# One chain per batch for the flow layer and the router of a two-layer decoder

## The chip, the cores and the metric

The kernel runs on one core of a Trainium2 chip. The core has five engines that run side by side, each with its own queue in strict order: TensorE (PE in the profile, with its weight loads as PEld), VectorE (DVE), ScalarE (ACT), GpSimd (POOL) and SyncE (SP), which here only starts transfers. The metric is the device time of one execution in microseconds, the median of several runs.

## The reference

Sixteen batches of 256 tokens with 256 channels go through two decoder layers: self-attention, cross-attention, a product-key layer, banded attention, the flow layer (`_L1_xattn_ref`) and a mixture of experts (`_L1_ffn_ref`). Each is applied to the layer norm of x, and its result is added to x. The last two are what the change touches (c is the normalised x, q is the context of 120 rows):

```python
cq = jnp.einsum('bcd,bqd,d->bcq', c, q, w_cq) + b_cq
s = (c @ w_c + b_c)[:, :, None] + (q @ w_q + b_q)[:, None, :] + cq
a = jax.nn.softmax(s, axis=2)
c2q_att = jnp.einsum('bcq,bqd->bcd', a, q)
b_att = jax.nn.softmax(jnp.max(s, axis=2), axis=1)
q2c_att = jnp.einsum('bc,bcd->bd', b_att, c)[:, None, :]
x = jnp.concatenate([c, c2q_att, c * c2q_att, c * q2c_att], axis=-1)
z = x @ W_l.T + b_l
...
logits = jnp.einsum('bsd,de->bse', input_emb, Wr) + br
route_w = jax.nn.softmax(logits, axis=-1)
_, topk_idx = jax.lax.top_k(route_w, TOP_K)
mask = jax.nn.one_hot(topk_idx, E, dtype=route_w.dtype).sum(-2)
routed = route_w * mask
routed = routed / routed.sum(axis=-1, keepdims=True)
h = jax.nn.relu(jnp.einsum('bsd,edh->ebsh', input_emb, W1) + b1[:, None, None, :])
expert_out = jnp.einsum('ebsh,ehd->ebsd', h, W2) + b2[:, None, None, :]
return jnp.einsum('bse,ebsd->bsd', routed, expert_out)
```

There are eight experts, and each token goes to the best two. All is float32.

## The kernel before

x stays in SBUF as sixteen tiles `xt[b]` of 128 partitions x 2 x 256. The layers follow one another, each over all batches. A framework places the instructions of an engine by what they depend on and adds the waits; inside a `manual_schedule` block, the engines named there keep the order of the program.

**Flow layer (L871 to L964).** `layernorm_stats` (L98 to L102) takes the statistics of all 32 halves of batches. Then a loop runs over the batches: two loads, `cx` (L883) and `cT` (L885), by SP; `qc` (L889) on DVE; the row of context terms `pr` (L894) and `qrow` (L896); the normalised x (L108), its transposes (L131) and their copy (L132); for each half, the scores `p_s` (L143, L145), their maximum `nm` (L906), the exponential `e` (L909), its scaling (L911), transpose (L913) and copy (L914); the attended context `pc` (L917); the second softmax over the maxima (`pm` L930, `low` L932, `be` L935, `pb` L940, `batt` L942), `pd` (L946) and `q2c` (L954). Four pairs of channel blocks form `xcat`: x, attended context (L924), their product (L925) and x scaled by `q2c` (L956). For each half, the output is a bias product (L959) and eight products with `wl` (L961), added to x by L964. A float32 product of 256 columns shows as two matrix instructions. `wl` itself is loaded ahead of the attention before it (L818).

**Router (L971 to L1080).** The statistics again, all 32 halves into one tile `xr` (L1009), transposes (L131), and products of eight columns, for each half a bias row (L143) and two channel blocks (L145). When those of all batches are there, the softmax (L1022 to L1027), the best two experts (`max` L1031, `max_index` L1032, `pick` L1038, `either` L1043) and the ranks are worked out for all tokens at once: two products of 256 columns (L1048) and a running sum over the 32 halves on DVE (`ahead`, L1052 to L1058). `place` is a token's row in the scratch array `rows`, where each expert has a region of 4096 rows, and `sloti` the same as an integer (L1078).

**Scattering (L1085).** Sixty-four indirect transfers on POOL's queue, each of 128 rows of 1040 bytes, write `xr` to `rows`. Beside them DVE works out the list of 39 tiles of 256 tokens: `full` (L1096), `need`, `ends` (L1107), `et`, the integer `eti` (L1123), and the rows that each tile gathers (`source`, L1145).

**Output biases (L1149 to L1158).** For each half, the routing weights are transposed (L1150), copied (L1152) and multiplied with `b2` (L1154); the result is added to x (L1155), and SP writes the batch to the output (L1158).

**Experts (L1161 on).** For each tile SP reads the expert's number and loads its weights `wt`, 2052 KB, into one of two buffers (L1165); POOL gathers the tokens from `rows` (L1173); then transposes (L1180), 16 + 16 products (L137, L1211), and an accumulating scatter to the output (L1220).

Of the kernel before, what the change touches and what calls it, by code (L numbers as in the profile page):

```python
# [12 lines left out]
U32 = mybir.dt.uint32  # L13
# [5 lines left out]
P = 128  # L19
# [32 lines left out]
def tile_decoder(ctx: ExitStack, tc: tile.TileContext, a: dict, out: bass.AP, last: int = 6):  # L52
# [762 lines left out]
    with ExitStack() as st:  # L815
        w4 = pool(st, "w4")
        wl = T(w4, [P, 8, D], "wl")
        nc.sync.dma_start(wl, a["l1x_w"].rearrange("(c p) e -> p c e", p=P))  # L818
        s4 = st.enter_context(ExitStack())
        w5 = pool(s4, "w5")  # L820
# [11 lines left out]
        wk = pool(s4, "wk4", 2)  # L832
        ps = pool(s4, "ps4", 2, PSUM)
        ps2 = pool(s4, "sc4", 1, PSUM)
# [36 lines left out]
        s4.close()  # L871
        if last == 4:
            return done()

        wk = pool(st, "wk5", 2)

        ps = pool(st, "ps5", 2, PSUM)
        layernorm_stats(wk)
        bsum = T(w4, [1, 1], "bsum")
        nc.vector.tensor_reduce(bsum, row(R_SC, 3), AX.X, ALU.add)  # L880
        for b in range(B):
            cx = T(wk, [NQ, D], "cx")
            nc.sync.dma_start(cx, a["ctx"][b])  # L883
            cT = T(wk, [P, 2, NQ], "cT")
            nc.sync.dma_start(cT, a["ctxT"][b].rearrange("(c p) q -> p c q", p=P))  # L885

            qc = T(wk, [P, 2, NQ], "qc")
            for dc in range(2):
                nc.vector.tensor_scalar(  # L889
                    qc[:, dc, :], cT[:, dc, :], col(C_WCQ + dc), col(C_WC + dc), ALU.mult, ALU.add  # L890
                )
            pr = T(ps, [1, NQ], "row")
            for dc in range(2):
                nc.tensor.matmul(pr, lhsT=col(C_WQ + dc), rhs=cT[:, dc, :], start=dc == 0, stop=dc == 1)  # L894
            qrow = T(wk, [1, NQ], "qrow")
            nc.vector.tensor_scalar(qrow, pr, bsum, None, ALU.add)  # L896

            xn = normalized(wk, b)
            xcat = T(wk, [P, 8, S], "xcat")
            transposed(ps, xn, xcat[:, 0:2, :])  # L900
            nm = T(wk, [P, 2], "nm")
            aT = T(wk, [NQ, 2, P], "aT")
            for t in range(2):
                p_s = T(ps, [P, NQ], "t2")
                project_rows(p_s, xcat, slice(t * P, (t + 1) * P), qc, 0, NQ, qrow)
                nc.vector.tensor_reduce(nm[:, t : t + 1], p_s, AX.X, ALU.max, negate=True)  # L906
                e = T(wk, [P, NQ], "e")
                z = T(wk, [P, 1], "z")
                nc.scalar.activation(e, p_s, AF.Exp, bias=nm[:, t : t + 1], accum_out=z)  # L909
                nc.vector.reciprocal(z, z)  # L910
                nc.vector.tensor_scalar(e, e, z, None, ALU.mult)  # L911
                pt = T(ps, [NQ, P], "t1")
                nc.tensor.transpose(pt, e, ident)  # L913
                nc.scalar.copy(aT[:, t, :], pt)  # L914
            pc = T(ps, [P, 2, S], "t2")
            for dc in range(2):
                nc.tensor.matmul(  # L917
                    pc[:, dc, :],
                    lhsT=cx[:, dc * P : (dc + 1) * P],
                    rhs=aT.rearrange("p t n -> p (t n)"),  # L920
                    start=True,
                    stop=True,
                )
            nc.scalar.copy(xcat[:, 2:4, :], pc)  # L924
            nc.vector.tensor_tensor(xcat[:, 4:6, :], xcat[:, 0:2, :], pc, ALU.mult)  # L925


            pm = T(ps, [1, 2, P], "row")
            for t in range(2):
                nc.tensor.matmul(pm[:, t, :], lhsT=nm[:, t : t + 1], rhs=ident, start=True, stop=True)  # L930
            low = T(wk, [1, 1], "low")
            nc.vector.tensor_reduce(low, pm, AX.XY, ALU.min)  # L932
            be = T(wk, [1, 2, P], "be")
            bz = T(wk, [1, 1], "bz")
            nc.scalar.activation(be, pm, AF.Exp, bias=low, scale=-1.0, accum_out=bz)  # L935
            nc.vector.reciprocal(bz, bz)
            nc.vector.tensor_scalar(be, be, bz, None, ALU.mult)
            pb = T(ps, [P, 2], "row")
            for t in range(2):
                nc.tensor.matmul(pb[:, t : t + 1], lhsT=be[:, t, :], rhs=ones[:, 0:1], start=True, stop=True)  # L940
            batt = T(wk, [P, 2], "batt")
            nc.vector.tensor_copy(batt, pb)  # L942
            pd = T(ps, [P, 2], "row")
            for dc in range(2):
                for t in range(2):
                    nc.tensor.matmul(  # L946
                        pd[:, dc : dc + 1],
                        lhsT=xn[:, t, dc * P : (dc + 1) * P],
                        rhs=batt[:, t : t + 1],
                        start=t == 0,  # L950
                        stop=t == 1,
                    )
            q2c = T(wk, [P, 2], "q2c")
            nc.vector.tensor_copy(q2c, pd)  # L954
            for dc in range(2):
                nc.vector.tensor_scalar(xcat[:, 6 + dc, :], xcat[:, dc, :], q2c[:, dc : dc + 1], None, ALU.mult)  # L956
            for t in range(2):
                y = T(ps, [P, D], "t2")
                nc.tensor.matmul(y, lhsT=ones, rhs=row(R_BL, D), start=True, stop=False)  # L959
                for c in range(8):  # L960
                    nc.tensor.matmul(  # L961
                        y, lhsT=xcat[:, c, t * P : (t + 1) * P], rhs=wl[:, c, :], start=False, stop=c == 7
                    )
                nc.vector.tensor_add(xt[b][:, t, :], xt[b][:, t, :], y)  # L964
    if last == 5:
        return done()
# [5 lines left out]
    with ExitStack() as st:  # L972
        w6 = pool(st, "w6")
        ws = pool(st, "ws", 2)
        wk = pool(st, "wk6", 2)
        s6 = st.enter_context(ExitStack())
        ps = pool(s6, "ps6", 2, PSUM)

        wr = T(w6, [P, 2, NE], "wr")
        nc.scalar.dma_start(wr, a["m_wr"].rearrange("(c p) e -> p c e", p=P))  # L980
        b2 = T(w6, [NE, D], "b2")
        nc.scalar.dma_start(b2, a["m_b2"])

# [14 lines left out]
        before_me = T(w6, [P, P], "before_me")  # L998
        nc.vector.tensor_scalar(before_me, along, part, None, ALU.is_gt)
        all_ones = T(w6, [P, P], "all_ones")  # L1000
        nc.vector.memset(all_ones, 1.0)

        layernorm_stats(wk)
        xr = T(w6, [P, NT, RW], "xr")
        pl = T(ps, [P, NT, NE], "lg", bufs=1)
        for b in range(B):
            for t in range(2):
                i = 2 * b + t
                nc.vector.tensor_scalar(  # L1009
                    xr[:, i, 0:D], xt[b][:, t, :], mv[:, i, 0:1], rstd[:, i : i + 1], ALU.subtract, ALU.mult  # L1010
                )
            xT = T(wk, [P, 2, S], "xT")
            transposed(ps, xr[:, 2 * b : 2 * b + 2, 0:D], xT)
            for t in range(2):
                project_rows(pl[:, 2 * b + t, :], xT, slice(t * P, (t + 1) * P), wr, 0, NE, row(R_BR, NE))

        def over(tile_):
            return tile_.unsqueeze(2).to_broadcast([P, NT, NE])

        red = T(w6, [P, NT], "red")  # L1020
        rw = T(w6, [P, NT, NE], "rw")
        nc.vector.tensor_reduce(red, pl, AX.X, ALU.max)  # L1022
        nc.vector.tensor_tensor(rw, pl, over(red), ALU.subtract)
        nc.scalar.activation(rw, rw, AF.Exp)
        nc.vector.tensor_reduce(red, rw, AX.X, ALU.add)
        nc.vector.reciprocal(red, red)
        nc.vector.tensor_tensor(rw, rw, over(red), ALU.mult)  # L1027
        top = T(w6, [P, NT, 8], "top")
        topi = T(w6, [P, NT, 8], "topi", U32)
        for i in range(NT):  # L1030
            nc.vector.max(out=top[:, i, :], in_=rw[:, i, :])  # L1031
            nc.vector.max_index(out=topi[:, i, :], in_max=top[:, i, :], in_values=rw[:, i, :])  # L1032
        first = T(w6, [P, NT, 2], "first")
        nc.vector.tensor_copy(first, topi[:, :, 0:2])
        picks = []
        for k in range(2):
            pick = T(w6, [P, NT, NE], f"pick{k}")
            nc.vector.tensor_tensor(  # L1038
                pick, over(first[:, :, k]), iota8.unsqueeze(1).to_broadcast([P, NT, NE]), ALU.is_equal
            )  # L1040
            picks.append(pick)
        either = T(w6, [P, NT, NE], "either")
        nc.vector.tensor_add(either, picks[0], picks[1])  # L1043


        pr = T(ps, [P, 2, NT, NE], "rank", bufs=1)
        for i, w in enumerate((before_me, all_ones)):
            nc.tensor.matmul(pr[:, i], lhsT=w, rhs=either, start=True, stop=True)  # L1048
# [298 lines left out]
```

## Time and profile before

| | us |
|---|---|
| three runs | 3927.28, 3928.51, 3930.91 |
| profiled execution | 3936.24 |
| its span, first to last instruction | 3934.5 |
| end of attention (last x add, L386), from the span's start | 2851.3 |
| first cx load of the flow layer | 2851.4 |
| first scores p_s of the flow layer | 2871.0 |
| last x add of the flow layer (L964) | 3161.2 |
| integer list of tiles eti | 3258.6 |
| first load of wt issued | 3260.9 |
| last scatter issued (L1085) | 3334.2 |
| first expert product (L137) | 3346.7 |

Over the whole span PE is busy for 3504.4 us, DVE 2275.2, POOL 1589.4 and ACT 1538.1. A busy PE is not a PE at its peak: products are pipelined and their ends are modelled, and TensorE's clock is granted in steps, so the same product takes twice as long at half clock. A row of the windows gives, for a stretch of the span, the busy time of each engine with its number of instructions, then TensorE's granted clock, the share of time in which the DMA engines were busy, and what they moved. A row of a timeline gives start, duration, engine, line, operation, output and inputs, and in brackets how long the engine was idle before and what ended that.

### The profile page before, as it was taken

The numbers are of one execution on the slowest core, as the hardware profiler recorded it, in microseconds if no ns is written. First come the engines' busy times: TensorE is split into PE (matmuls) and PEld (weight loads), VectorE is DVE, ScalarE is ACT, GpSimd is POOL, SyncE is SP. The second block draws the span as 40 slices with busy tenths as digits, with TensorE's granted clock in tenths as the row PEclk, the third lists the DMA queues.
The fourth block names the chain that finished last, engine by engine and source line by source line (L and its number), as shares of the span: only waits on it lengthen the run. The fifth ranks groups of instructions, "written<-read, shape, count | busy, mean of one in ns | idle before, by whom it ended". The sixth has DMA issues, their size and how long they took to land.

```text
span 3934.5 us, 130886 instructions
## 1 busy us (share of the span) xinstructions
PE 3504.4 (89%) x57612; PEld 2876.7 (73%) x57612; DVE 2275.2 (58%) x9061; ACT 1538.1 (39%) x2704; POOL 1589.4 (40%) x1551
## 2 busy tenths in 40 slices
PE   6999999659999999999999987999879983999998
PEld 3666777448888888888888875676556671788887
DVE  6777533498888888888888733444343331111111
ACT  2455566434444444444444324555411110232232
POOL 2333200036666666666666633444300006233332
PEclk8999999879999999999999997999889855999999
DMA  9200000200000000000000000000000004465564
GB/s 334 86 2 2 5 9 8 93 3 4 4 4 4 4 4 4 4 4 4 4 4 4 4 27 1 1 2 2 2 17 14 11 6 171 141 190 178 172 187 132
DMA packets 49325, 182.00 MB, mean 46 GB/s; under 512 B 14889, under 2 KB 36785, under 8 KB 42354
## 3 DMA queue, kind: packets, MB, share of 16 engines
q1 hardware_dynamic: 29840, 144.22, 10.4%
q0 software_dynamic: 18048, 29.14, 3.5%
q8 instruction: 452, 7.41, 0.8%
q14 instruction: 119, 0.97, 0.1%
q10 hardware_dynamic: 866, 0.26, 0.0%
HBM read 150.66 MB, written 57.15 MB: 53 GB/s over the span
## 4 chain that ended last, share of the span: by engine, by line
PE 66%; DVE 25%; POOL 3%; ACT 3%; issue 2%; another core or an unknown queue 1%; DMA 0%; ACTq 0%; POOLq 0%; DVEq 0%
PE acc L758 8%; PE sa L246 7%; PE h L137 7%; PE t L145 7%; DVE hot L714 7%; PE y L1211 7%; PE hid L137 6%; PE t L733 4%; PE t L961 3%; PE t L347 3%; POOL hot L721 3%; DVE q L274 2%; PE t L137 2%; PE t L228 2%; PE sb L246 2%
## 5 line engine op out<-in xcount | busy, mean ns | idle before, releaser
L721 POOL TENSOR_TENSOR hot<-hot,w 104x1024 f32<-104x1024 f32 x256 | 523.1, 2043 | 295.9 <-DVE hot L714 192.0
L714 DVE TENSOR_TENSOR hot<-wij,iota 104x1024 f32<-104x1024 f32 x512 | 599.2, 1213 | 52.9 <-ACT w L704 44.0
L137 PE MATMUL hid<-xnT,w_dn 128*128 128x128 f32 x4096 | 525.3, 281 | 5.5 <-issue 5.3
L137 PEld LDWEIGHTS hid<-xnT,w_dn 128*128 128x128 f32 x4096 | 483.8, 193 | 17.9 <-issue 8.3
L758 PE MATMUL acc<-w_up,hg 128*128 128x256 f32 x2048 | 482.3, 381 | 0.0
L274 DVE TENSOR_REDUCE q<-sa 128x4 f32<-128x1024 f32 (+1 forms) x192 | 231.1, 1204 | 429.7 <-PE sb L246 248.1
L752 POOL TENSOR_TENSOR hg<-hg,gate 128x512 f32<-128x512 f32 x256 | 342.0, 1336 | 238.5 <-ACT hg L751 235.8
L246 PE MATMUL sa<-kT,qT 32*128 32x256 f32 (+2 forms) x3072 | 350.8, 355 | 90.3 <-DVE q L274 60.7
L733 PEld LDWEIGHTS t<-hot,hot 104*32 104x32 f32 x32768 | 309.1, 110 | 156.4 <-POOL hot L721 114.7
L733 PE MATMUL t<-hot,hot 104*32 104x32 f32 x32768 | 339.1, 199 | 89.2 <-POOL hot L721 86.3
L758 PEld LDWEIGHTS acc<-w_up,hg 128*128 128x128 f32 x2048 | 372.2, 190 | 42.6
L315 ACT ACTIVATE pT<-sb 128x1024 f32<-128x1024 f32 (+1 forms) x288 | 294.8, 1024 | 276.6 <-PE sb L246 238.0
L246 PEld LDWEIGHTS sa<-kT,qT 32*128 32x128 f32 x3072 | 240.9, 192 | 172.0 <-DVE q L274 93.5
L740 ACT COPY gate<-t 128x512 f32<-128x512 f32 x256 | 270.7, 1057 | 244.9 <-PE t L733 244.8
L246 PE MATMUL sb<-qmT,kT 32*128 32x256 f32 (+2 forms) x2560 | 344.8, 391 | 7.7 <-ACT pT L315 7.2
L137 PE MATMUL h<-xT,wt 128*128 128x256 f32 x1248 | 283.1, 385 | 13.2 <-ACT hT L1207 7.2
L326 POOL TENSOR_TENSOR pT<-pT,bandf 128x260 f32<-128x260 f32 x256 | 184.0, 740 | 249.3 <-ACT pT L315 249.3
L1211 PE MATMUL y<-wt,hT 128*128 128x256 f32 x1248 | 276.0, 379 | 0.4 <-DVE ys L1219 0.4
L751 ACT ACTIVATE hg<-hid 128x512 f32<-128x512 f32 x256 | 153.7, 600 | 305.7 <-PE hid L137 305.3
L137 PEld LDWEIGHTS h<-xT,wt 128*128 128x128 f32 x1248 | 226.3, 192 | 63.7 <-ACT hT L1207 13.0
L1220 POOL DMA_INDIRECT out_y<-ys,toi x78 | 123.1, 1578 | 344.1 <-DVE ys L1219 303.1
L1211 PEld LDWEIGHTS y<-wt,hT 128*128 128x128 f32 x1248 | 237.0, 190 | 33.0 <-DVE ys L1219 0.8
(281 smaller groups left out, 5803.9 us busy)
## 6 DMA issues: line engine op xcount, KB each, us to landing
wt<-in_m_w SPq DMA_DIRECT2D x39, 2052.0 KB
rows<-in_zeros SPq DMA_DIRECT2D x32, 1040.0 KB
x<-in_x SPq DMA_DIRECT2D x16, 256.0 KB
w_dn<-in_p_dn SPq DMA_DIRECT2D x2, 2048.0 KB
w_up<-in_p_up SPq DMA_DIRECT2D x1, 4096.0 KB
out_y<-x SPq DMA_DIRECT2D x16, 256.0 KB
cT<-in_ctxT SPq DMA_DIRECT2D x32, 120.0 KB
cx<-in_ctx SPq DMA_DIRECT2D x16, 120.0 KB
```

The source lines that it names most:

```text
L137: nc.tensor.matmul(o, lhsT=w[:, dc, c0 : c0 + n], rhs=rhs[:, dc, :], start=dc == 0, stop=stop and dc == 1)
L145: nc.tensor.matmul(o, lhsT=xT[:, dc, tok], rhs=w[:, dc, c0 : c0 + n], start=bias is None and dc == 0, stop=dc == 1)
L246: nc.tensor.matmul(sc[0 : ls.stop - ls.start, r, g, 0 : rs.stop - rs.start], lhsT=lhs[rows_, g0 + g, ls], rhs=rhs[rows_, g0 + g, rs], star ...
L274: nc.vector.tensor_reduce(to, sc[:, :, :, 0:nk], AX.X, ALU.max)
L315: nc.scalar.activation(pT[0:kn], sc[0:kn], AF.Exp, scale=1.0 / math.sqrt(DH))
L714: nc.vector.tensor_tensor(t, wij[:, k, cs].unsqueeze(2).to_broadcast([HS, NC, PK]), iota[0:HS].unsqueeze(1).to_broadcast([HS, NC, PK]), AL ...
L721: nc.gpsimd.tensor_tensor(hot[1], hot[1], w[:, cs].unsqueeze(2).to_broadcast([HS, NC, PK]), ALU.mult)
L733: nc.tensor.matmul(pg[q * NLO : (q + 1) * NLO, t, :], lhsT=hi[:, t, i0 : i0 + NLO], rhs=hj[:, t, j0 : j0 + NLO], start=True, stop=True,)
L740: nc.scalar.copy(gate[:, :, c * NC : (c + 1) * NC].rearrange("p l t -> p t l"), pg)
L752: nc.gpsimd.tensor_tensor(hg, hg, gate[:, s * L : (s + 1) * L, :], ALU.mult)
L758: nc.tensor.matmul(acc, lhsT=hg[:, i, :], rhs=w_up[:, l, :], start=l == 0, stop=l == NLO - 1)
L1211: nc.tensor.matmul(y, lhsT=hT[:, fc, h * P : (h + 1) * P], rhs=w2[:, fc, :], start=fc == 0, stop=fc == FF // P - 1,)
```

## The change

Flow layer, routing, ranks, scattering and output biases become one generator, `flow(b)`, and TensorE's order is that of the program: every third turn a new batch joins, and in each turn every batch that is in work, oldest first, goes on to its next `yield`. In the steps of a batch:

1. context loads three batches ahead (eight buffers), layer norm through `fresh` (statistics of four batches at a time), the flow bias `badd` added to x on POOL, `qc` on POOL, transposes
2. the row of context terms
3. scores of both halves, one maximum, exponentials, the scaling of e by ACT
4. maxima transposed, their softmax
5. e transposed for both halves at once
6. `batt`, with the scaling by `bz` in the product
7. attended context `att`, and `both`
8. `q2c`, and `wb`: the weights of the first and last channel blocks are combined on DVE, so that six products do for eight
9. first half of the output, six products and no bias product
10. second half; added to x; statistics, a square root for this batch alone, and the normalised x by ACT
11. transposes
12. router products, first part of the softmax
13. rest of the softmax, best two
14. ranks, with `free` carrying the ends of the experts' regions from batch to batch in place of the running sum; four scatters; transposes of the weights
15. b2 products, x added, output written

`wl` is loaded after the attention, at the head of this stage, and the pool of `wt` is opened when the chain's pools are closed. `count` is taken from `free` at the end; the list of tiles and the experts are as before.

```diff
-        w4 = pool(st, "w4")
-        wl = T(w4, [P, 8, D], "wl")
-        nc.sync.dma_start(wl, a["l1x_w"].rearrange("(c p) e -> p c e", p=P))
...
+        wk = pool(s6, "wk5", 4)
+        ps = pool(s6, "ps5", 2, PSUM)
...
+        free = [T(w6, [P, 2, NE], "free0")]
+        nc.vector.tensor_copy(free[0][:, 0], regions)
...
+        def flow(b):
...
+            xn = fresh(wk, b)
+            nc.gpsimd.tensor_tensor(xt[b], xt[b], badd.unsqueeze(1).to_broadcast([P, 2, D]), ALU.add)
...
-                nc.vector.tensor_scalar(
+                nc.gpsimd.tensor_scalar(
                     qc[:, dc, :], cT[:, dc, :], col(C_WCQ + dc), col(C_WC + dc), ALU.mult, ALU.add
                 )
...
+            wb = T(wk, [P, 2, D], "wb")
             for dc in range(2):
-                nc.vector.tensor_scalar(xcat[:, 6 + dc, :], xcat[:, dc, :], q2c[:, dc : dc + 1], None, ALU.mult)
-            for t in range(2):
-                y = T(ps, [P, D], "t2")
-                nc.tensor.matmul(y, lhsT=ones, rhs=row(R_BL, D), start=True, stop=False)
-                for c in range(8):
+                nc.vector.scalar_tensor_tensor(
+                    wb[:, dc, :], wl[:, 6 + dc, :], q2c[:, dc : dc + 1], wl[:, dc, :], ALU.mult, ALU.add
+                )
+            yield
+            y = T(ps, [P, 2, D], "y")
+            for t in range(2):
+                parts = [(u, w, c) for u, w in ((att, wl[:, 2:4]), (both, wl[:, 4:6]), (xnT, wb)) for c in range(2)]
+                for i, (u, w, c) in enumerate(parts):
                     nc.tensor.matmul(
-                        y, lhsT=xcat[:, c, t * P : (t + 1) * P], rhs=wl[:, c, :], start=False, stop=c == 7
+                        y[:, t], lhsT=u[:, c, t * P : (t + 1) * P], rhs=w[:, c, :], start=i == 0, stop=i == 5
                     )
...
+            std = T(wk, [P, 2], "std2")
+            nc.scalar.activation(std, mv[:, ts, 1], AF.Sqrt, bias=eps)
+            nc.vector.reciprocal(rstd[:, ts], std)
+            shift = T(wk, [P, 2], "shift")
+            nc.vector.scalar_tensor_tensor(shift, mv[:, ts, 0], -1.0, rstd[:, ts], ALU.mult, ALU.mult)
+            for t in range(2):
+                i = 2 * b + t
+                nc.scalar.activation(
+                    xr[:, t, 0:D], xt[b][:, t, :], AF.Identity, bias=shift[:, t : t + 1], scale=rstd[:, i : i + 1]
+                )
+            yield
...
+            pr = T(ps, [P, 2, 2, NE], "row")
+            for i, w in enumerate((before_me, all_ones)):
+                nc.tensor.matmul(pr[:, i], lhsT=w, rhs=either, start=True, stop=True)
+            now = free.pop()
+            then = T(w6, [P, 2, NE], f"free{(b + 1) % 2}")
+            free.append(then)
+            nc.vector.tensor_add(now[:, 1], now[:, 0], pr[:, 1, 0])
+            nc.vector.tensor_add(then[:, 0], now[:, 1], pr[:, 1, 1])
...
+            for t in range(2):
+                for k in range(2):
+                    ins = nc.gpsimd.indirect_dma_start(
...
+            y = T(ps, [P, 2, D], "y")
+            for t in range(2):
+                nc.tensor.matmul(y[:, t], lhsT=rT[:, t, :], rhs=b2, start=True, stop=True)
+            nc.vector.tensor_add(xt[b], xt[b], y)
+            nc.sync.dma_start(out[b * S : (b + 1) * S, :].rearrange("(t p) d -> p t d", p=P), xt[b])
+
+        with tc.manual_schedule(engines={mybir.EngineType.PE}):
+
+            going, turn = [], 0
+            while going or turn < 3 * B:
+                if turn % 3 == 0 and turn < 3 * B:
+                    going.append(flow(turn // 3))
+                going = [g for g in going if next(g, 0) is None]
+                turn += 1
...
+        count = T(w6, [P, NE], "count")
+        nc.vector.tensor_sub(count, free[0][:, 0], regions)
+        s6.close()
         ws = pool(st, "ws", 2)
         wk = pool(st, "wk6", 2)
```

## The prediction

> **What bounds it now.** I read the page's forty slices first, then cut the stretch which the change touches into windows, then the chain of waits inside it.
>
> ```profile
> PE   6999999659999999999999987999879983999998
> ...
> POOL 2333200036666666666666633444300006233332
> PEclk8999999879999999999999997999889855999999
> ```
>
> TensorE (PE) is busy nearly everywhere; only slice 34 (3246 to 3344 us) is a third full, at half clock, while POOL works; slice 33 before it is also at half clock.
>
> ```profile
> core 0: us, PE busy (x) PEld busy (x) DVE busy (x) ACT busy (x) POOL busy (x), PEclk, DMA share, GB/s
> 2851.40:3161.30 309.90, 275.23 (x1248) 200.33 (x1248) 123.97 (x466) 51.82 (x163) 0.00 (x0) 0.87 0.05 13
> 3161.30:3223.70 62.40, 59.41 (x256) 57.30 (x256) 12.04 (x39) 12.25 (x19) 0.96 (x8) 0.53 0.01 1
> 3223.70:3253.60 29.90, 18.62 (x41) 8.46 (x42) 23.69 (x156) 3.64 (x14) 0.00 (x0) 0.50 0.13 44
> 3253.60:3337.80 84.20, 29.54 (x60) 11.60 (x59) 12.78 (x40) 4.83 (x19) 62.31 (x64) 0.50 0.47 163
> 3337.80:3346.70 8.90, 2.04 (x9) 1.40 (x9) 2.13 (x18) 0.59 (x1) 6.68 (x7) 0.50 0.77 304
> 3346.70:3372.20 25.50, 18.32 (x66) 15.09 (x66) 3.45 (x22) 4.19 (x9) 4.52 (x5) 0.75 0.11 22
> 3372.20:3934.50 562.30, 547.45 (x2581) 465.55 (x2579) 95.98 (x430) 163.82 (x341) 188.23 (x145) 1.00 0.58 173
> ```
>
> Five stages follow one another: flow layer 309.9, router products 62.4, ranks 29.9, scattering 84.2, first gather 8.9. From the end of attention (2851.4) to the first expert product (3346.7) that is **495.3 us**. In none of them do two engines share the load: in the first two PE carries it, then DVE, then POOL. The expert stage behind is PE work at full clock and is not touched.
>
> ```profile
> 3253.64 1.22 POOL L1085 DMA_INDIRECT rows<-xr,sloti  x1 [90.98 <-DVE x L1155]
> 3255.16 0.98 POOL L1085 DMA_INDIRECT rows<-xr,sloti  x1 [0.30 <-issue]
> ```
>
> This is the timeline of POOL. The 64 scatters stand 1.28 us apart (0.98 and 0.30), and none starts before 3253.6, when the ranks of all tokens are known: 64 x 1.28 = 82 us in which no other engine has work that decides. The chain of waits shows the same: pieces of 6 to 8 us of "another core or an unknown queue" from 3282 on. They delay only the output biases (L1150 to L1158), which end before the last scatter does.
>
> **The change, part by part.** Each batch becomes one chain of 15 steps (14 yields). A new batch starts every third turn, so by my count five, not six, are in work. TensorE's order is fixed: in each turn the oldest batch goes first.
>
> *TensorE work.* The cx loads of the flow loop at 2990.01, 3006.55 and 3023.09 give 16.54 us a batch at clock 1.00. Half an output (L959, L961) is 18 instructions; the sixteen products are issued in 3.44, 0.215 each, and the bias takes 0.62. Twelve products take 2.58, so 1.48 a half, 3.0 a batch are saved. About 1.7 of the 16.54 is waiting (0.86 for e, 0.70 for qrow and smaller ones), which interleaving can hide: 16.54 - 3.0 - 1.7 = 11.8. Added are the router's transposes and products, 3.65 a batch in the second window at half clock, 1.9 at full; ranks with 16 instead of 256 columns 0.5; transposes of rw 0.25; b2 products, four instructions, 0.95. **15.4 us at full clock.**
>
> *The clock.* The flow averaged 18.08 a batch (271.2 us from 2890 to 3161.3, 15 batches), 1.09 times its best. Here rule and row differ. The Trainium skill, "TensorE: Matmul & The Clock Gate", section "What's actually happening", says that the gate opens after about 3.4 us of sustained activity and closes after an idle window. The second window has PE 95% busy and still 0.53: eight-column products without gaps held it at half. By the rule, a chain without gaps runs at 15.4; by that row, at 30.8. Most of the mixture is the flow's own products, so I take the flow's row: 15.4 x 1.09 = **16.8**.
>
> *Waits on TensorE.* The tight place is step 10 to 11: after the last y product come the x add (0.68 by L925, same size), two bn_stats (0.87 the pair with aggregates), a table load (1.28), the square root (0.2), reciprocal and shift (0.4) and two 128x256 activations (0.8), with handovers about 4.6. TensorE meanwhile has steps 7, 4, 1 and 14: 1.06 + 0.5 + 0.5 + 0.75 = 2.8, with gaps 3.1. So 1.5 a batch remain. For the other boundaries (the ring of two "row" banks that six steps share, DVE and ACT in queue order) no row exists: bounds 0 and 6; I take 1.4, near the 1.7 that one batch alone waits. **Period 16.8 + 1.5 + 1.4 = 19.7 us.**
>
> *Table loads.* The Sqrt of each batch now stands between Exps. A rule speaks against it: "ScalarE: Activation LUTs", section "Table sets: the hidden batching unit", wants all calls of one set done before switching, and "What ACT_TABLE_LOAD costs" puts a switch at 2.66 us, 1.28 load plus 1.38 drain. ACT's own timeline in the flow's first batch:
>
> ```profile
> 2870.38 0.58 ACT L132 COPY xcat<-t 128x512 f32<-128x512 f32 x1 [2.21 <-PE t L131]
> 2870.98 1.28 ACT L909 ACT_TABLE_LOAD   x1
> ```
>
> The load starts 0.02 after the copy ends: no drain is seen. By the row two switches a batch, and two more in each fourth, cost 3.2 on ACT, by the page 6.7. ACT's other work is some 6.8 (exp with readout 1.1, three 128x512 copies 1.75, be 0.64, two e scalings 0.7, two xr 0.8 and small ones), so 10.0 or 13.5 of 19.7: hidden either way. On the step 10 path the page would add 1.4 a batch, 22 us in all. I take the row.
>
> *Other engines.* DVE, by rows of the same shapes: 12 us a batch (statistics twice 1.7, xn 0.7, x adds 1.4, both 0.7, wb 0.8, maxima, low, qrow and reciprocals 1.6, the 26 small router and rank operations 5.0). POOL: four scatters 5.1, badd 1.5 and qc 0.7 by L326's 0.74 for 260 columns, iota 0.15: 7.4. Both are below 19.7. qc can stand behind four scatters, 5.1 us, and is needed two turns later (13 us). The carried ends (now, then) wait for the batch before, which is three turns ahead: nothing; without that cover 0.3. The output writes and ctx loads move to SP beside the chain: 256 and 240 KB per 19.7 us, with scatters some 50 GB/s where the trace has shown 304. wl's load moves from under attention (issued at 2317) to the head of SP's queue: 1 MB at 304 GB/s is 3.4 us ahead of cT, which landed at 2854.2 before and then at 2858. The first xnT comes only about 2860, so nothing; without that cover 3.4.
>
> *Filling and draining.* There are 60 turns. The first twelve have one to four batches and are ruled by latency: 12 us for the first three (statistics of eight instead of 32 tiles, which bring the first p_s from 2871 to 2861), then 7, 11 and 16: 46. The last twelve: 15, 13, 11 and 5: 44. Between lie 12 periods x 19.7 = 236. Counts are known at 2851.4 + 326 = 3178.
>
> *The tail.* The list of tiles (full to eti, some 15 serial DVE operations of 0.15 to 0.48) takes 4.5, with the rest of step 14 5.5; from eti to the load of wt 2.1 (3258.74 to 3260.85); 2.05 MB at about 290 GB/s 7, landing 2; ws now lies in the chain's memory, so wt can wait for the last scatter: 2. Sum 19, first expert product at 3197. Before, this load was hidden behind the scatters; it is **late next**. The four last scatters (5.1) and the first gather (7) run beside it.
>
> **Sum:** 46 + 236 + 44 + 19 = 345 against 495.3: 150 less. The expert stage keeps its start-up. The profiled run took 3936.24 (span 3934.5 and 1.7 around it), becoming 3786. The timed median, 3928.51, lies 7.7 lower: **3778 us**.
>
> **Rivals.**
> - *Dense* (0.17): the interleaving covers all waits and holds the clock near 1: period 16.5, filling 80: 12 x 3.2 + 10 = 48 less, 3730. For it: clock 1.00 in several flow batches. Against: fixed order on TensorE and step 10.
> - *A chain of handovers* (0.20): DVE and ACT serve five batches in queue order, each step comes a few us late, and the 15 steps give a period of 25: 64 more and 15 on filling, 3857. For it: DVE at 12 of 19.7 with 40 operations a batch. Against: the first window's waits for DVE and ACT are mostly below 1 us.
> - *Half clock, slower* (0.08): the small products in each turn keep the clock at half. PE work is 30.8, filling and draining 135, so 12 x 30.8 + 135 + 19 = 524, 29 more than 495.3: 3957. It decides from (495.3 - 19 - 135) / 12 = 28.4 us a batch, clock 0.54. For it: the router's 0.53. Against: the flow at 0.87 with the same y products, which remain two thirds as many.
> - That scattering isn't covered: 4 x 1.28 fits any period above 7.4, so only a stall of TensorE beside it, as from 3270 to 3333, could bring it back; thirteen scatters from 3254 to 3270 left the 1.45 us steps alone.
>
> **Numbers.** The forecast itself has 0.55; its own range (period 18 to 22) is 3758 to 3806. The range of 3720 to 3860 takes in the dense and the handover case. About 0.2% (8 us) is what the measurement can tell from no change. Faster 0.90, within 0.2% 0.02, slower 0.08.
>
> **What would show it.** Right: no stretch with POOL alone; wr products between y products; about 20 us from one scatter group to the next; first expert product near 3197 with TensorE waiting for wt; clock 0.85 to 0.95 there. Wrong: more than four table loads a batch, a clock near 0.5 in mid-chain, xT transposes waiting over 4 us for xr, or TensorE waiting for row banks at each turn.

## The result: 38 us less, not 150, and the profile after

Before: 3927.91 us (3927.28 to 3930.91, four runs). After: **3889.53 us** (3884.99 to 3895.38, four runs). Ratio 0.9902, 95% interval 0.9884 to 0.9919. The profiled run took 3884.99, its span is 3883.3. Line numbers are now those of the changed kernel, or of the experiment that is named.

First the page's slices, the three rows that were read before:

```profile
PE   6999999749999999999999998999878786999998
...
POOL 2333200036666666666666652444422212333332
PEclk8999999969999999999999997999976776999999
```

The stretch with POOL alone and PE at 3 is gone. But where the chain runs, PE stands at 7 or 8 and its clock at 6 or 7, lower than the flow layer had before. The windows of the changed kernel say it more exactly: filling, the middle, draining, the tail and the experts (columns as in the prediction's windows: length, busy time of PE, PEld, DVE, ACT and POOL, PE's clock, DMA share, GB/s).

```profile
2845.20:2900.00 54.80, 41.58 (x172) 30.42 (x172) 20.68 (x83) 18.55 (x47) 12.63 (x27) 0.66 0.29 70
2900.00:3225.50 325.50, 264.49 (x1134) 210.49 (x1133) 140.38 (x629) 117.06 (x268) 72.80 (x90) 0.71 0.10 34
3225.50:3281.90 56.40, 41.99 (x167) 34.33 (x165) 23.64 (x128) 17.82 (x32) 11.98 (x14) 0.70 0.12 43
3281.90:3305.10 23.20, 4.57 (x13) 2.27 (x12) 10.49 (x52) 0.95 (x2) 12.00 (x13) 0.50 0.68 261
3305.10:3883.30 578.20, 563.12 (x2646) 478.95 (x2645) 99.25 (x453) 168.48 (x350) 191.82 (x148) 0.99 0.56 169
```

From the end of attention (2845.2) to the first expert product (3305.1) it takes 459.9 us: 35.4 less than the 495.3 of before, where 345 was forecast. Two more pieces make up the 51.2 between the two spans: the experts take 578.2 instead of 587.8 (9.6), and attention, whose code is the same, ended 6.1 earlier in this run (in other runs of this study it ended between 2847 and 2859).

In the middle, one batch follows the other after **26.7 us** instead of 19.7: the attended context of batch 2 starts at 2905.20, that of batch 14 at 3225.52, twelve periods in 320.3. What such a period consists of is seen in four windows of TensorE, which follow one another:

```profile
3048.30:3057.00 8.70, 8.68 (x34) 7.05 (x35) 3.47 (x6) 1.48 (x4) 3.52 (x4) 0.50 0.22 76
3057.00:3060.20 3.20, 3.20 (x9) 2.63 (x10) 2.42 (x18) 0.21 (x1) 0.00 (x0) 0.56 0.00 1
3060.20:3068.90 8.70, 8.70 (x51) 6.73 (x49) 3.75 (x14) 2.73 (x9) 0.87 (x2) 1.00 0.00 1
3068.90:3073.40 4.50, 0.08 (x2) 0.04 (x1) 1.51 (x11) 4.44 (x9) 2.00 (x2) 1.00 0.08 30
```

PE works 8.7 us without a gap on small products (transposes, one, eight or 120 columns, and the four of `b2`), all at half clock (the same four instructions of y take 2.05 us at half clock and 1.03 at full, as the rows under e2 show); then 3.2 us on the first half of y, still nearly all at half clock; then 8.7 us at full clock, with 51 products where the first window had 34; then it waits 4.5 us, and it all begins again. The timeline of the same kernel, all engines, shows what it waits for (start, duration, engine, line, operation; in brackets the idle time before it and what ended that):

```profile
3066.21 1.03 PE L990 MATMUL t<-aT,cx 120*128 120x256 f32 x4
3066.48 0.69 DVE L1030 TENSOR_TENSOR x<-x,y 128x512 f32<-128x512 f32 x1 [1.23 <-PE y L1025]
...
3067.96 0.66 DVE L1000 TENSOR_TENSOR both<-xnT,t 128x512 f32<-128x512 f32 x1
...
3068.53 0.18 DVE L1038 BATCH_NORM_AGGREGATE mv<-bnst 128x2 f32<-128x6 f32 x1
...
3068.98 0.36 ACT L1135 COPY rT<-t 8x256 f32<-8x256 f32 x1
...
3069.36 1.28 ACT L1040 ACT_TABLE_LOAD   x1
...
3070.65 0.29 ACT L1040 ACTIVATE std<-mv,eps 128x2 f32<-128x2 f32 x1
...
3070.96 1.28 ACT L973 ACT_TABLE_LOAD   x1
...
3072.26 0.47 ACT L973 ACTIVATE be<-row,low 1x256 f32<-1x256 f32 x1
...
3072.72 1.07 ACT L1046 ACTIVATE xr<-x,shift,rstd 128x256 f32<-128x256 f32 x2
...
3073.36 1.39 PE L131 MATMUL t<-ident,xr 128*128 128x128 f32 x4 [4.42 <-ACT xr L1046]
```

From the last y product (3066.4, when the x add starts) to the transposes are 7.0 us, not 4.6. On DVE, `both` of a younger batch (0.66) stands ahead of the second aggregate, which ends at 3068.71. ACT is busy with copies until 3069.34 and turns to the square root, with its table load, only then; and between the square root (until 3070.94) and the norm that needs it (from 3072.72) stands `be` of a younger batch, an exponential, with a table load of its own: 1.78 us that belong to another chain. The second wait, once in four batches, is for `xn`: the statistics of eight halves at once. In the view of waits, for PE from 2900 to 3200 (total, times, longest):

```profile
PE t L131 <- ACT xr L1046: 35.5, 9, 4.4
PE t L131 <- DVE xn L108: 20.7, 3, 6.9
```

And POOL's timeline, where 64 scatters stood in a row before:

```profile
3050.63 0.16 POOL L1116 IOTA xr<- 128x2 f32 x1
...
3070.92 1.02 POOL L1122 DMA_INDIRECT rows<-xr,sloti  x1 [6.17 <-DVE sloti L1114]
3072.24 0.97 POOL L1122 DMA_INDIRECT rows<-xr,sloti  x1 [0.30 <-issue]
```

The scatters come four by four with POOL idle between the groups: they are hidden, as forecast.

### The profile page after: what moved, and what is told of

It reads as the page before. It is cut to its first block, busy times and chain, and to the rows that moved or that the text cites. A ratio compares the mean times of both kernels' runs of the same rounds, so it can differ in the third digit from the quotient of the medians.

```text
span 3883.3 us, 131076 instructions
## 1 busy us (share of the span) xinstructions
PE 3469.4 (89%) x57482; PEld 2873.8 (74%) x57482; DVE 2288.9 (59%) x9235; ACT 1621.8 (42%) x2837; POOL 1629.0 (42%) x1614
## 5 line engine op out<-in xcount | busy, mean ns | idle before, releaser
L137 PEld LDWEIGHTS hid<-xnT,w_dn 128*128 128x128 f32 x4096 | 483.5, 192 | 17.7 <-issue 7.6
```

Of the source, the lines that this page charges most:

```text
L137: nc.tensor.matmul(o, lhsT=w[:, dc, c0 : c0 + n], rhs=rhs[:, dc, :], start=dc == 0, stop=stop and dc == 1)
```

## The experiments

Two causes are in question: the waits, and the clock. Theory "clock" came out of the windows above: TensorE is granted the full clock only while wide products (256 columns) come often enough, and any stretch of a few microseconds with nothing, or with small products alone, loses it. By turns, y's halves fall to two neighbouring turns and the third turn (ranks, xT, q2c, e, qrow) has small products only. The rival is that waits alone set the period. The runs are on several chips, so each time is given as a ratio to the kernel before on the same chip (it took 3924 to 3936 there), with its interval. In the diffs the minus lines are those of the changed kernel.

### One more turn between norm and transposes (e1)

```diff
             yield
+            yield
             xT = T(wk, [P, 2, S], "xT")
```

> One more turn between step 10 (xr) and step 11 (its transposes); nothing else. Theory A (one gap and the clock): in the changed kernel TensorE stands still once a batch, 4.4 to 4.7 us for xr, and the 10 to 12 us behind the gap run at half clock; warm work is 14.7 us. With a whole turn of cover the gap goes, the clock rises from 0.70 to 0.9 or more, the period falls from 25 to 15.5 to 17.5 us: 12 full periods x 8 = 95 us and a part of the filling, less some 5 us for the added turn: 3770 to 3810 us. Theory B (many handovers in the queues of DVE and ACT): other waits take the gap's place, period 22 to 24, 3850 to 3880. Theory C (the mixture of small products holds the clock at 0.70 whatever the gaps): only the gap goes, period 20 to 21, 3825 to 3845, clock still about 0.7.

Measured: **0.9835** (0.9804 to 0.9867). The period falls from 26.7 to 24.7 us. The wait for xr falls from 35.5 to 13.7 us in the 300 (longest 2.3) and isn't gone, others of 6.8 (`qrow`) and 6.1 (`aT`) come up, and the clock rises only from 0.71 to 0.75. The wait is part of the cause, not all of it.

### The gap filled with useless wide products (e2)

```diff
-            transposed(ps, xr[:, :, 0:D], xT)
...
+            for _ in range(10):
+                nc.tensor.matmul(pf[:, 0:D], lhsT=wl[:, 2, 0:P], rhs=wl[:, 3, :], start=True, stop=True)
+            for dc in range(2):
+                for t in range(2):
+                    nc.tensor.transpose(pt[:, dc, t, :], xr[:, t, dc * P : (dc + 1) * P], ident)
...
```

(The lines with `transpose` are what `transposed` did; `pf` is a view of their PSUM tile.)

> Ten products of 256 columns whose result is overwritten stand ahead of the transposes of step 11, so that TensorE is busy while xr is made; at full clock they take 4.3 us, about the gap. The path from the last y product to xr stays as it is. Theory A: the gap is filled, the clock no longer falls, period 14.7 + 4.5 = 19 to 20 us instead of 25: 60 to 80 us less than the changed kernel, 3810 to 3830, clock 0.9 or more. Theory C: the clock stays near 0.7, the filler then takes 6 to 8 us instead of 4.3, the period grows by 2 to 4: 3920 to 3950. Theory B: no difference beyond 10 us.

Measured: **0.9825** (0.9801 to 0.9849). Some 4.4 us of work that nobody needs is added to every batch, and the kernel is faster than the change. Outside the batches with the wait for `xn` the period is 22.7. The clock still falls once a period. A window of this run, from behind the dummies to the first y product, and the timeline at its end:

```profile
3068.62:3073.82 5.20, 5.07 (x35) 4.24 (x35) 1.81 (x4) 1.46 (x4) 2.10 (x3) 0.95 0.23 80
```

```profile
3072.24 0.61 PE L145 MATMUL row<-wr,xT 128*128 128x8 f32 x4
...
3073.09 0.88 PE L145 MATMUL row<-wr,xT 128*128 128x8 f32 x4
3073.82 2.05 PE L1025 MATMUL y<-wl,att 128*128 128x256 f32 x4
3075.67 1.53 PE L1025 MATMUL y<-wl,both 128*128 128x256 f32 x4
3077.04 1.03 PE L1025 MATMUL y<-wb,xnT 128*128 128x256 f32 x4
```

PE is busy for 5.07 of 5.20 us, without one wait; yet four router products go from 0.61 to 0.88, and the four instructions of y from 1.03 to 2.05. It is not idleness that takes the clock here; what stands ahead of the fall is some 4.5 us of small products (among them the four instructions of `b2`, 1.12 us, with 256 columns but eight rows only). It comes back after 3.2 us of y, in the cycle before after 5.3.

### The norm on VectorE (e3)

```diff
-                nc.scalar.activation(
-                    xr[:, t, 0:D], xt[b][:, t, :], AF.Identity, bias=shift[:, t : t + 1], scale=rstd[:, i : i + 1]
-                )
+                nc.vector.tensor_scalar(
+                    xr[:, t, 0:D], xt[b][:, t, :], mv[:, i, 0:1], rstd[:, i : i + 1], ALU.subtract, ALU.mult
+                )
```

> The normalised x of step 10 is written by DVE (0.37 each half) instead of ACT, where it stood behind a second table load and the exponential be. The path shortens by about 1.3 to 2 us, so the gap falls from 4.5 to about 2.5 to 3.2. Theory A [...]: most of the half-clock stretch goes too, period 17 to 19, 3780 to 3830. Theory A with a clock that falls in proportion, or B: only the gap's 1.3 to 2 us a batch, 20 to 30 us, 3855 to 3870. Theory C: the same 20 to 30 us at an unchanged clock.

Measured: **0.9841** (0.9812 to 0.9871). (`shift` falls away.) xr no longer queues behind `be` and its table load: the longest wait falls from 4.4 to 2.8, so the second load, `be`, `shift` and the norm's longer time on ACT cost 1.6 on the path together. The clock stays at 0.72.

### Six products alone, in the kernel before (b1)

```diff
-                for c in range(8):
+                for c in (2, 3, 4, 5, 0, 1):
                     nc.tensor.matmul(
-                        y, lhsT=xcat[:, c, t * P : (t + 1) * P], rhs=wl[:, c, :], start=False, stop=c == 7
+                        y, lhsT=xcat[:, c, t * P : (t + 1) * P], rhs=wb[:, c, :] if c < 2 else wl[:, c, :],
+                        start=False, stop=c == 1,
```

(`wb` is made as in the change; the bias product stays.)

> The kernel before with six instead of eight products (wb from q2c on DVE, bias product kept), everything else as before. By the sum of the prediction four instructions of 0.215 us fewer in each half, 1.7 us a batch, 27 us: 3900. Rival: the dense part of a batch shrinks while its 8 us of small products stay, so the clock of the flow falls below 0.87 and gives back 10 to 25 us: 3910 to 3930.

Measured: 0.9977 (0.9959 to 0.9996), a third of what was expected. The windows from the second batch's attended context to the last one's, this run (fifteen periods) and then the kernel before (fourteen):

```profile
2883.47:3154.86 271.39, 257.13 (x1049) 179.27 (x1048) 104.69 (x369) 46.24 (x150) 0.00 (x0) 0.79 0.05 13
```

```profile
2889.87:3143.01 253.14, 237.21 (x1094) 173.30 (x1093) 95.55 (x346) 43.31 (x141) 0.00 (x0) 0.91 0.05 13
```

The period is 18.09 us with six products and 18.08 with eight. A quarter of the wide products is gone, the small ones between them are the same, and the granted clock falls from 0.91 to 0.79: in this execution the saving was taken back in full. It is one of the slower ones (3942.10, where twenty lie between 3904 and 3948 with a median of 3929.24); over all of them a third of the expected saving is left. Over the whole span the clock of the twenty is 0.928 to 0.939, that of 23 executions of the kernel before on the same chip 0.935 to 0.942.

### Statistics ahead of their need (e4)

```diff
-            xn = fresh(wk, b)
+            xn = normalized(wk, b)
+            soon(b + 4)
```

(`soon`, called ahead of the loop for batches 0 to 3, takes the statistics of the two halves of the batch four later, and for every fourth the square root of eight.)

> Only the layernorm statistics of the next four batches move: two tiles in each batch's first step instead of eight tiles at every fourth, and the square root one batch early. The change's own kernel stood at 0.990 of the kernel before. Theory 'stalls': TensorE's three waits for xn of 6.9 us each (20.7 us) go and nothing takes their place, 0.985. Theory 'vector queue': the same 14 us of DVE work now delays every batch's short steps, so nothing is won, 0.990. Theory 'clock': three idle windows fewer also lift the mean clock of 0.71 a little, 0.983.

Measured: 0.9878 (0.9862 to 0.9895); the change's own kernel stood at 0.9902 and, run again as e8, at 0.9918 (0.9896 to 0.9940). The waits for xn are gone, those for xr have become more (40.1 us in 250, eleven times). The period is 25.9: of the 20.7 us, some 12 x 0.8 = 10 were won. By the ratios alone the intervals touch.

### y in three turns (e5), and the fourth corner (e9)

```diff
-                if t == 0:
-                    yield
+                    if 6 * t + i in (3, 7):
+                        yield
...
             yield
+            yield
             xT = T(wk, [P, 2, S], "xT")
```

> The twelve products of y in three groups of four, one in each of three turns, and one more turn between the norm and its transposes: same work, 17 steps instead of 15. Theory 'clock' [...]: no turn holds small products alone any more, the clock from 2900 to 3200 rises from 0.71 to over 0.85 and the period falls from 24.4 to about 17.5 us, some 95 us less over 14 periods, 12 more for two more steps in filling: ratio about 0.969. Theory 'waits only': the wait for xr goes as it did with one more turn alone, the clock stays near 0.75, period 22, ratio 0.983.

Measured: **0.9678** (0.9659 to 0.9697). Not an instruction is added or taken away against e1: the twelve products of y are spread over three turns, four in each. The window of its twelve periods:

```profile
2899.26:3130.94 231.68, 217.20 (x1102) 170.77 (x1101) 123.48 (x606) 110.77 (x259) 69.97 (x87) 0.85 0.13 45
```

The clock is at 0.85 and the period at 19.3 us. e9 is the same without the additional turn:

> The fourth corner beside after (neither), e1 (one more turn before the transposes, 0.9835) and e5 (both, 0.968): y in three turns, but the transposes in the turn right after the norm. After the last y product TensorE then has 2.6 us of small work against the path's 7, so the wait for xr stays at about 4 us a batch. Theory 'clock and wait are two causes': wide products come right behind the gap and in every turn, the clock rises to about 0.78, the period to some 22 us, ratio 0.980 to 0.984. Theory 'the gap alone sets the clock': as long as the 4 us gap is there, nothing is won, ratio 0.990.

Measured: 0.9847 (0.9820 to 0.9875), period 23.9, clock 0.74, in the slowest of its four executions (3853 to 3878). The wait for xr stays (4.1 at the longest), as expected, but the clock rises less. So the two causes don't add: one more turn alone takes 2.0 us off the period, y in three turns alone 2.8, both together 7.4. In the single periods the clock is 0.69 to 0.79 with e1, 0.70 to 0.89 with e9, 0.74 to 1.00 with e5. The three turns change more than the clock, though: the waits for `xn`, 20.7 us in 300 in the changed kernel and in e1, are gone in e9 and 2.5 us in e5. Why they go is not shown. Of the 5.4 us between the periods of e1 and e5, 2.8 are idle time of PE and 2.6 its busy time.

### A second filler (e6)

```diff
             pt = T(ps, [NQ, 2, P], "t1")
+            pf = pt.rearrange("p t n -> p (t n)")
+            for _ in range(8):
+                nc.tensor.matmul(pf, lhsT=wl[:, 2, 0:NQ], rhs=wl[:, 3, :], start=True, stop=True)
```

(on top of e2.)

> The ten dummy products of 256 columns ahead of the xr transposes as in e2, and eight more ahead of the transposes of e, in the middle of the stretch of small products; both results are overwritten. Theory 'clock': with wide products in every 4 us the clock from 2900 to 3200 goes from 0.84 (e2) to over 0.93, and although 1.7 us of useless work a batch is added, the period falls from 22.8 to about 19.5: ratio 0.972. Theory 'waits only': useless work costs what it takes, 1.7 to 3.4 us a batch more than e2, ratio 0.99 to 0.995.

Measured: 0.9883 (0.9867 to 0.9900). The clock did what "clock" says, the time did not: I had put eight dummies at 1.7 us, one instruction each, and they show as two. The timeline of one period:

```profile
3054.74 4.58 PE L1057 MATMUL t<-wl 128*128 128x256 f32 x20
3059.17 0.94 PE L1060 MATMUL t<-ident,xr 128*128 128x128 f32 x4
...
3060.76 3.69 PE L979 MATMUL t<-wl 128*120 128x256 f32 x16
3064.29 0.38 PE L981 MATMUL t<-ident,e 128*120 128x128 f32 x2
...
3078.22 4.58 PE L1057 MATMUL t<-wl 128*128 128x256 f32 x20
```

The dummies hold PE for 4.43 and 3.53 us, 7.96 of a period of 23.48. The rest, **15.5 us**, is a batch's real work at full clock, with 0.2 us idle: what the prediction had put at 15.4. The window of this period, and that of one with the wait for `xn`, show the clock:

```profile
3054.74:3078.22 23.48, 23.26 (x128) 19.06 (x128) 11.44 (x49) 8.89 (x22) 6.38 (x8) 1.00 0.10 36
2915.41:2949.92 34.51, 27.60 (x129) 22.65 (x128) 17.30 (x69) 11.77 (x24) 9.04 (x9) 0.80 0.09 31
```

With a wait of 6.9 us such a period is 11.0 us longer: PE's own work, of the same products, takes 27.6 us instead of 23.3.

### Towards a better version (e7, e10, e11)

e7 is e5 with the statistics of e4:

> The two edits together: y in three turns with the later transposes, and statistics two tiles at a time. If stall and clock are separate causes, the gains add: about 0.005 to 0.007 below y in three turns alone. If TensorE is no longer what ends the period (DVE has 44% of the flow now, ACT 36%), the second edit brings nothing on top.

Measured: 0.9657 (0.9640 to 0.9673); period 19.3 as in e5. On e5 alone it wins 0.002, less than expected, with touching intervals. e10 adds one `yield` ahead of the rank products, e11 also the norm on VectorE (the edit of e3):

```diff
             yield
+            yield
 
             pr = T(ps, [P, 2, 2, NE], "row")
```

> y in three turns with the statistics ahead (0.9657), and one more turn between the router's softmax and the rank products: 18 steps. TensorE's waits there (L1114 and L1151, 14.5 us in 250) and the half clock that followed them go; one more turn in filling costs about 5 us. Theory 'clock': clock from 2900 to 3100 from 0.85 to over 0.92, period from 19.3 to about 17.5, ratio about 0.962. If DVE's queue sets the period, the waits only move to another tile and the ratio stays at 0.966.

> As e10, with the norm's two activations on VectorE (as in e3). With two turns of slack behind the norm, ACT's two table loads are off the path already: same as e10 within 0.002. If ACT's queue still delays the copies that TensorE waits for, 0.002 to 0.004 below e10.

e10: 0.9671 (0.9646 to 0.9696), nothing that can be told from e7: the waits went, as expected, but the clock in its profile was 0.79 instead of higher. Its runs lie further apart (3785 to 3815) than those of the others, and the profiled one was the slowest (span 3813.3), so its clock need not be that of the rest. Within this profile, with one order of products throughout, the periods run from 16.27 us at 0.98 to 25.34 at 0.61; this is left open. e11: **0.9613** (0.9593 to 0.9634), 3770.51 us beside 3887.89 for the change and 3923.85 for the kernel before on the same chip. Its twelve periods:

```profile
2903.19:3118.32 215.13, 212.93 (x1096) 166.95 (x1094) 129.43 (x606) 95.36 (x233) 68.29 (x82) 0.85 0.14 47
```

PE is hardly idle any more: 2.2 us in twelve periods of 17.9. Yet its clock is 0.85, as in e5. Two of these periods, one right behind the other:

```profile
2956.56:2976.72 20.16, 20.16 (x94) 15.95 (x92) 12.58 (x49) 10.34 (x22) 8.02 (x9) 0.75 0.17 53
2976.72:2992.06 15.34, 15.34 (x94) 12.33 (x93) 10.92 (x57) 7.48 (x19) 5.35 (x8) 1.00 0.18 60
```

Both have the same 94 matrix instructions in the same order, and neither has a wait. One loses the clock, the other doesn't, and takes 15.34 us, the prediction's sum without any dummies. The flow loop before did the same; two of its periods, again with one order of products:

```profile
2948.56:2970.62 22.06, 20.89 (x79) 15.11 (x78) 6.88 (x25) 3.05 (x10) 0.00 (x0) 0.74 0.04 12
2988.84:3005.38 16.54, 15.37 (x79) 11.23 (x78) 6.88 (x25) 3.05 (x10) 0.00 (x0) 1.00 0.06 16
```

So theory "clock" holds as a tendency, not as a rule: the order of the products makes a loss more or less frequent, and what decides in the single period is not shown.

That e11 gains 0.0058 on e10, more than either expectation allowed, speaks for ACT's queue, which is 11% less busy; but within the two intervals it can also be 0.004 or less, so this cause is argued, not shown. e8, the control:

> The changed kernel itself once more, beside the three others on one chip: 0.990 of the kernel before, as in the result. If it comes to 0.988 here, then moving the statistics alone (0.988 on another chip) has won nothing that can be told from a chip's spread; at 0.990 it has won some 8 us of the 20.7 that the three stalls held.

Measured: 0.9918, as in the result. Beside it e4's 0.9878, on another chip, fits the 10 us that e4's trace shows, but the intervals leave it open whether it was less.

The main runs in one table, over the twelve periods from the attended context of batch 2 to that of batch 14; idle is the stretch less PE's busy time:

| | period | PE idle | PE busy | granted clock | ratio |
|---|---|---|---|---|---|
| forecast | 19.7 | 2.9 | 16.8 | 0.85 to 0.95 | 0.962 |
| after | 26.7 | 5.1 | 21.6 | 0.71 | 0.990 |
| e1, one more turn | 24.7 | 4.0 | 20.7 | 0.75 | 0.9835 |
| e9, y in three turns | 23.9 | 3.5 | 20.5 | 0.74 | 0.9847 |
| e5, both | 19.3 | 1.2 | 18.1 | 0.85 | 0.9678 |
| e10 | 19.8 | 0.6 | 19.2 | 0.79 | 0.9671 |
| e11 | 17.9 | 0.2 | 17.7 | 0.85 | 0.9613 |

## Why the prediction was wrong

- **What bounds it, and the scattering:** right. Its 84 us are hidden.
- **TensorE's work of 15.4 us a batch:** right; 15.5 by e6, 15.34 by a period of e11.
- **The clock, "15.4 x 1.09 = 16.8":** this is the step that failed most. The busy time of a period is 21.6, so the factor is 21.6 / 15.5 = 1.39: 6.1 us lost to half clock, where I had 1.4. I took the flow's own factor because "most of the mixture is the flow's own products". But this factor does not stay with the products: the change took a quarter of y's away (b1, where only that was done, showed 0.79 instead of 0.91 in one of its slower executions) and put new small products together into one turn, and the same instructions in another order (e1 and e5) ran at 0.75 and 0.85. Nor was it one factor in the flow itself, whose periods went from 16.54 to 22.06 us. The rule of the Trainium skill, "TensorE: Matmul & The Clock Gate", section "What's actually happening", was the other side of my choice: sustained activity opens the gate. It doesn't cover this case as I put it, "a chain without gaps runs at 15.4": 8.7 us without gaps stayed at 0.50 here, e2 lost the clock in a stretch that was 97% busy, and 20.16 us of e11 without a gap ran at 0.75. The row of the router stage, 0.53 at 95% busy, was the nearer one for a turn of small products, and I used it only for a rival. (It is not eight-column products alone, as I read it: 17.7 of its 59.4 us are transposes.)
- **Waits, "1.5 a batch remain" and "1.4":** together 2.9 forecast, 5.1 measured. I had named the place, step 10 to 11, and the sign ("xT transposes waiting over 4 us for xr"), but mis-sized the path: 7.0 us, not 4.6. What lacked was the queues' other work: `both` on DVE ahead of the second aggregate, the copies on ACT ahead of the square root, and `be` with a second load between the square root and the norm. And a wait costs more than its length (by 1.2 to 4.1 us in e6), for which the sum had no term. There nine of the twelve periods have hardly a wait (some 0.2 us idle) and take 23.48 us at full clock, but for one of 25.16 at 0.93; the three with the wait of 6.9 us for `xn` take 31.57 to 34.51 at 0.80 to 0.89.
- **Table loads, "hidden either way":** true of ACT's busy time (9.6 us a batch, forecast 10.0), wrong of the path. The rule of the Trainium skill, "ScalarE: Activation LUTs", section "Table sets: the hidden batching unit", to do all of one set before the other, did bear on this change, though not by the drain: the load after the square root starts 0.02 us after it. It bore by a second load on the path, which I had counted off it.
- **Other engines:** DVE 11.7 us a batch (forecast 12), POOL 6.0 (7.4): right, neither is the bound.
- **Filling 46, draining 44, tail 19:** 60, 56 and 23. Filling and draining ran at 0.66 and 0.70. In the tail TensorE did not wait for wt, as I had put it, but for the first gather: this was issued at 3292.0, once its list `source` was there (3291.1), its rows came until 3304.9, and TensorE waited for them four times.
- **"The expert stage keeps its start-up":** it became 9.6 us shorter. Before, its first eight products were followed by a wait of 7.2 us; in the changed kernel the first 32 follow one another without one.

The sum: 60 + 320 + 56 + 23 = 460, against 345; of the 115, twelve periods hold 84, and those are 12 x (4.7 clock + 2.2 waits). Of the rivals, the chain of handovers (period 25, 3857 us) came nearest, but in part by luck: its period holds 25 - 16.8 = 8.2 us of waits, and 5.1 were measured. Its reason was only half of it: DVE and ACT in queue order explain the waits, and a mean clock of 0.71, half-way from the flow's 0.87 to the 0.54 of the half-clock rival, explains the rest. I had held the two apart; they come together. That the same chain, with its turns cut otherwise, can do what was forecast is shown by e5 and e11: periods of 19.3 and 17.9, and in e11 338 us from attention (2853.7) to the first expert product (3191.9), where the forecast had 345.

## What to carry to other kernels

When independent chains are woven into one fixed order for TensorE, filling every gap isn't enough: look at where several us hold small products alone (e2 lost the clock behind 4.5 us of them), and give such a stretch its share of wide products, by splitting a long accumulation over turns if need be. Cost a wait or a run of small products with the half clock that follows it, and a saving of wide products with the clock that it may take away. For a handover between engines, write out the queue of each engine on the path, the work of other chains included, and give the longest one a turn of slack before tuning anything else.

## What the hardware showed unexpectedly

A busy TensorE lost its clock. In the changed kernel 34 small products in 8.70 us, PE busy for 8.68, ran at 0.50 throughout; in e2 the clock fell behind some 4.5 us of small products, with 5.07 of 5.20 us busy. It came back after 3.2 to 5.3 us of products with 256 columns. Adding dummy products of that width in two places raised it from 0.71 to 0.94 over twelve periods. Yet the order of the products alone doesn't settle it: of two neighbouring periods of e11 with the same instructions, one held the full clock and one fell to 0.75 on average, behind 2.7 us of small products (2962.66 to 2965.37). What differed between the two is not shown. Which property of a product counts, its columns, its rows, or the share of time in which the array takes in data, these runs don't tell apart.
